# Start of a decoder layer on one Trainium2 core: the keys' weight ahead of half the tokens, exchanges ahead of the second keys, key groups in another order

## The chip, the cores and the metric

The kernel runs on one core of one Trainium2 chip. The metric is the device time of one execution in microseconds. The numbers in the views below come from one profiled execution; its own time and the times of unprofiled runs stand in the table further down.

## The reference

The reference is one layer of a pre-norm decoder in float32, on x of 4 batches x 1024 tokens x 512 features: self-attention with 16 heads of 32 features and sigmoid gates, cross-attention to a context of 4 x 1024 x 384, and a small network, each added to its input. Only the start concerns the change. Cut to that:

```python
n = layernorm(x)                          # per token, over 512 features
inner = n @ Wi                            # "queries" of self-attention, 512 x 512
outer = n @ Wo                            # "keys", 512 x 512
v = n @ Wv                                # values, 512 x 512
aperture, expression = sigmoid(n @ Wa + ba), sigmoid(n @ We + be)
a = softmax(inner @ outer.T / sqrt(32)) * aperture * expression
x = x + rotate((a / a.sum(-1)) @ v) @ Wout
x = x + cross_attention(layernorm(x), ctx) ; x = x + network(layernorm(x))
```

## The kernel before, in words

All engines work from instruction lists whose order is written out by hand in the program: the order in which Python issues operations is the order on each engine. Waits between engines are placed by the framework from the tiles that instructions read and write. SyncE (SP) and ScalarE (ACT) each issue transfers on a queue of their own, GpSimd (POOL) on a third.

Work is cut into batches of 1024 tokens, halves of 512 tokens and tiles of 128 tokens. Batch by batch, self-attention runs for every half and every group of four heads over eight key tiles; preparation of the next batch is woven between its steps. Ahead of the first attention step stands a list `first`, which has nothing to be woven into: it prepares batch 0 on its own. The change lies in that list and in the transfers ahead of it.

**Transfers.** `x0` holds tokens 0 to 511 as four tiles `xin`. Lines 135 to 137 ask for the four tiles, even ones on SP, odd ones on ACT. Lines 138 and 139 then ask for the keys' weight `wk0` (`attn_Wo`, 512 x 512) by quarters: `by_quarters` sends each quarter to 32 partitions, two quarters on SP and two on ACT. A tile and a quarter both are 256 KB.

**First half of batch 0.** For each tile, VectorE (DVE) takes statistics (L401, L402), GpSimd makes the scale 1/sqrt(variance + eps) (L405, L406), and VectorE normalizes in place (L303). VectorE's order is: statistics of 0 and 1, normalization of 0, statistics of 2, normalization of 1, statistics of 3, normalizations of 2 and 3. Then the tile is exchanged (`tr`, `across`, L325): TensorE (PE) multiplies 16 blocks with the identity into a PSUM bank `f`, of which there are two, and ScalarE copies the bank back over the tile (L331), so that features lie on partitions. ScalarE's first copy has the load of an activation table ahead of it.

**Keys of the first half.** `k_tiles(t0, nt, gs)` makes the keys of tiles t0 to t0 + nt - 1 for the groups gs of 128 output features, with 16 matmuls for each group (`columns`, L87), into `me["pk"][g]`. These four places are the halves of two PSUM tiles `s`: groups 0 and 1 share one, groups 2 and 3 the other. When the last tiles of a group are done, VectorE copies the group out to `k` (L284). `first_k` sets the order: tile 0's keys are cut into groups (0, 1) and (2, 3), and stand between exchanges; tiles 1 to 3 follow in one call with all four groups.

**After the keys.** SP's next transfer, tokens 512 to 1023 (L381), waits for a small GpSimd copy (L380) behind the scale of tile 3; behind it come the queries' weight `Wi` (`attn_Wi`) and the values' weight (`attn_Wv`). Then the query groups (`q`, L87 into `f`), gates (L482), and the values follow. The gates' weights (`attn_Wa`, `attn_We`) are asked for on ACT's queue behind the four exchange copies.

Of the kernel before, what the change touches and what calls it, by code (L numbers as in the profile page):

```python
# [10 lines left out]
F32 = mybir.dt.float32  # L11
# [5 lines left out]
P = 128  # L17
B, T, D = 4, 1024, 512
H, DH = 16, 32
NPR = H // 2  # L20
HG = 4
NT = T // P
NC = D // P
# [19 lines left out]
@with_exitstack  # L43
def decoder_kernel(ctx: ExitStack, tc: tile.TileContext, a: dict, out: bass.AP):

    nc = tc.nc
    keep = ctx.enter_context(tc.tile_pool(name="keep", bufs=1))
    flag = keep.tile([1, 1], I32, name="flag")
    E = mybir.EngineType
    with tc.manual_schedule(engines={E.PE, E.DVE, E.Activation, E.Pool, E.SP}):
        moderate_path(tc, a, out, flag)
    again = nc.values_load(flag[0:1, 0:1], min_val=0, max_val=1, skip_runtime_bounds_check_because="0 or 1")
    with tc.If(again > 0):  # L60
        general_path(tc, a, out)


def moderate_path(tc: tile.TileContext, a: dict, out: bass.AP, flag: bass.AP):
    nc = tc.nc
    x = a["x"]
    with ExitStack() as st:
# [6 lines left out]
        wp = enter(tc.tile_pool(name="mwp", bufs=3))  # L74
# [8 lines left out]
        def columns(to, lhsT, rhs, **flags):  # L83

            for j in range(4):
                r = slice(j * DH, (j + 1) * DH)
                nc.tensor.matmul(to[r], lhsT=lhsT[:, j, :] if len(lhsT.shape) == 3 else lhsT[:, r], rhs=rhs, **flags)  # L87

        def by_quarters(dma, to, w):

            for q in range(NC):
                dma[q * len(dma) // NC](to[ts(q, NB)], w.rearrange("(q c i) f -> q i c f", c=NC, i=NB)[q])
# [15 lines left out]
        for one, is_ in ((ones, 1.0), (power, -0.5), (share, 1.0 / M)):  # L108
# [6 lines left out]
        W_IN = {  # L115
            "q0": (a["attn_Wi"], NC), "k0": (a["attn_Wo"], NC), "v0": (a["attn_Wv"], NC),
            "q1": (a["xattn_Wq"], NC), "k1": (a["xattn_Wk"], NCK), "v1": (a["xattn_Wv"], NCK),
            "o1": (a["xattn_Wo"], NC),
        }
# [13 lines left out]
        x0 = p2.tile([P, 4, D], F32, tag="inT", name="xin")  # L133

        queues = [nc.sync.dma_start, nc.scalar.dma_start]
        for t in range(4):
            queues[t % 2](x0[:, t, :], x[0, t * P : (t + 1) * P, :])
        wk0 = wp.tile([P, NC, D], F32, tag="w", name="w")
        by_quarters(queues, wk0, W_IN["k0"][0])
        wae = const.tile([P, NC, 2 * H], F32, name="wae")  # L140

        nbae = const.tile([P, 1], F32, name="nbae")
# [133 lines left out]
        def evacuate(to, src, bias=None):  # L276

            if crossing:
                if bias is None:
                    nc.scalar.copy(to, src)  # L280
                else:
                    nc.scalar.activation(to, src, AF.Identity, bias=bias)
            elif bias is None:
                nc.vector.tensor_copy(to, src)  # L284
            else:
                nc.vector.tensor_scalar(to, src, bias, None, ALU.add)
# [48 lines left out]
        def chunk(xt, c, t0=0, n=4):  # L335

            return xt[:, t0 : t0 + n, :].rearrange("p t (s c j) -> p (t s) c j", c=NC, j=NB)[:, :, c, :]
# [18 lines left out]
        def pre(u):  # L356
# [72 lines left out]
            def tr(hf, t):  # L429
                def f():  # L430
                    if xt0(hf):
                        xn = me["xn", hf]
                        across(xn, t, first=True)
                    else:
                        xn = me["xT", hf]
                        blocks(xn, t)
                    me["in", hf] = lambda c: chunk(xn, c)
                    me["in", hf, "t"] = lambda c, i: chunk(xn, c, i, 1)
                return f
# [112 lines left out]
            def k_tiles(t0, nt, gs):  # L552

                def f():
                    xn = me["xn", 0]
                    if "pk" not in me:
                        me["pk"] = [two[:, i, :] for two in (ps.tile([P, 2, HALF], F32, tag="s", name="s") for _ in range(2)) for i in range(2)]
                        me["k"] = p2.tile([P, NC, T], F32, tag="k", name="k")
                    for g in gs:
                        to = me["pk"][g][:, t0 * P : (t0 + nt) * P]  # L560
                        for c in range(NC):
                            columns(to, me["wk"][:, c, ts(g, P)], chunk(xn, c, t0, nt), start=(c == 0), stop=(c == NC - 1))
                        if t0 + nt == 4:
                            evacuate(me["k"][:, g, 0:HALF], me["pk"][g])
                return [(1, f)]

            def first_k():
                trs_ = [[(1, tr(0, t))] for t in range(4)]
                return [
                    trs_[0], k_tiles(0, 1, (0, 1)), trs_[1], k_tiles(0, 1, (2, 3)), trs_[2], trs_[3],  # L570
                    k_tiles(1, 3, range(HG)),
                ]

            vs = [values(kt) for kt in range(NT)]
# [1188 lines left out]
```

## Time and profile before

| what | us |
|---|---|
| median of 3 runs | 2198.9 |
| the three runs | 2198.63, 2198.9, 2202.58 |
| profiled execution, its own time | 2197.95 |
| span of the profiled execution | 2196.1 |
| TensorE busy in the span | 2169.3 |
| first query group starts, from the span's start | 29.26 |
| first attention step starts | 102.14 |

All times in the views count from the start of the span. A line of a timeline gives start, length, engine, source line, operation, written and read tiles, shape and count; a bracket tells how long the engine was idle before it and which instruction or transfer released it. "x32" counts matmuls as the chip records them: a float32 matmul appears twice. The length of a run of matmuls reaches to the modelled end of the last one, so that the next run starts 0.2 us or so before that; starts are the safer numbers. "SPq" and "ACTq" lines are the issuing of transfers, not their landing. Line numbers are those of the kernel before; in the changed kernel all lines behind the edited transfers (from 140 on) are one higher.

### The profile page before, as it was taken

How to read it: one execution, taken by the hardware profiler on the slowest of the kernel's cores; microseconds unless marked ns; L12 is line 12 of the kernel's file. 1: busy time of each engine (PE TensorE's matmuls, PEld its weight loads, DVE VectorE, ACT ScalarE, POOL GpSimd, SP SyncE). 2: the span in 40 equal slices, each digit the busy share in tenths (PEclk: the TensorE clock that was granted, in tenths of full speed). 3: DMA queues.
4: the chain of work that ended last, by engine and by line, in shares of the span. 5: the costliest groups of instructions: out<-in, count | busy, mean ns of one | idle time of the engine just before them, and what ended most of it. 6: DMA issues, size and time to landing. Idle time of an engine off the chain costs nothing.

```text
span 2196.1 us, 53076 instructions
## 1 busy us (share of the span) xinstructions
PE 2169.3 (99%) x22750; PEld 556.2 (25%) x22750; DVE 1558.7 (71%) x2510; ACT 1240.3 (56%) x1493; POOL 85.6 (4%) x127
## 2 busy tenths in 40 slices
PE   8999999999999999999999999999999999999996
PEld 4322222222222222222222222222222222222223
DVE  3578675796757957567676676877777777856477
ACT  0155545555455554555656666675757666577673
POOL 2000000030200000000000000000000000000000
PEclk9999999999999999999999999999999999999998
DMA  5412133031340221211222132221233142202131
GB/s 153 134 47 72 47 98 113 19 89 66 97 118 19 85 66 51 74 47 42 69 85 90 45 93 65 79 76 53 69 86 110 50 103 69 81 19 80 60 89 41
DMA packets 154137, 161.72 MB, mean 74 GB/s; under 512 B 47002, under 2 KB 92698, under 8 KB 152740
## 3 DMA queue, kind: packets, MB, share of 16 engines
q1 hardware_dynamic: 149828, 156.14, 24.5%
q8 instruction: 180, 2.95, 0.6%
q0 software_dynamic: 2080, 0.98, 0.3%
q10 hardware_dynamic: 1984, 1.12, 0.2%
q14 instruction: 65, 0.53, 0.1%
HBM read 115.40 MB, written 42.74 MB: 72 GB/s over the span
## 4 chain that ended last, share of the span: by engine, by line
PE 95%; DVE 2%; ACT 1%; issue 1%; DMA 0%; ACTq 0%; DVEq 0%
PE f L87 36%; PE s L607 26%; PE av L634 22%; PE sm L642 6%; PE sm L664 3%; ACT e L612 1%; PE s L87 1%; PE f L912 1%; PE f L874 1%; DVE g L901 1%; DVE es L620 0%; DMA w<-in_attn_Wo 0%; PE f L482 0%; PE s L912 0%; PE f L325 0%
## 5 line engine op out<-in xcount | busy, mean ns | idle before, releaser
L612 ACT ACTIVATE e<-s 128x1024 f32<-128x1024 f32 x1024 | 993.6, 1022 | 709.6 <-PE s L607 511.7
L620 DVE TENSOR_TENSOR es<-es,e 128x1024 f32<-128x1024 f32 x534 | 642.4, 1227 | 268.3 <-ACT e L612 266.4
L607 PE MATMUL s<-q,k 32*64 32x512 f32 x8192 | 607.2, 613 | 2.2 <-ACT e L612 0.5
L634 PE MATMUL av<-e,v 128*32 128x512 f32 x4096 | 550.2, 603 | 0.0
L87 PE MATMUL f<-xT,w 128*32 128x512 f32 x2816 | 333.7, 592 | 0.0
L628 DVE SCALAR_TENSOR_TENSOR eg<-e,sw,eg 128x512 f32<-128x512 f32 x448 | 318.5, 747 | 2.3
L618 DVE TENSOR_TENSOR es<-e 128x1024 f32<-128x1024 f32 x89 | 106.8, 1223 | 219.9 <-ACT e L612 188.0
L607 PEld LDWEIGHTS s<-q,k 32*64 32x64 f32 x8192 | 132.8, 129 | 445.8 <-ACT e L612 241.4
L87 PE MATMUL f<-w,q 128*32 128x512 f32 x1984 | 240.3, 592 | 0.0
L634 PEld LDWEIGHTS av<-e,v 128*32 128x32 f32 x4096 | 87.9, 108 | 403.9 <-issue 401.3
L87 PEld LDWEIGHTS f<-xT,w 128*32 128x32 f32 x2816 | 92.1, 110 | 210.5 <-issue 206.0
L642 PE MATMUL sm<-e,sw 128*2 128x512 f32 x1024 | 133.3, 592 | 0.0
L87 PE MATMUL f<-w,xT 128*32 128x512 f32 x896 | 106.0, 592 | 0.6 <-DVE q L284 0.6
L87 PEld LDWEIGHTS f<-w,q 128*32 128x32 f32 x1984 | 65.5, 110 | 149.1 <-issue 142.6
L87 PE MATMUL f<-w,ctxT 128*32 128x512 f32 x768 | 92.6, 592 | 0.0
L87 PE MATMUL f<-ctxT,w 128*32 128x512 f32 x768 | 92.3, 592 | 0.0
L895 ACT ACTIVATE hid<-sT,units 128x256 f32<-128x256 f32 x128 | 76.5, 605 | 27.8 <-DVE g L901 24.1
L811 POOL TENSOR_TENSOR r<-res,bo_bc 128x512 f32<-128x512 f32 x32 | 40.9, 1279 | 1040.8 <-DVE res L803 703.4
L901 DVE SCALAR_TENSOR_TENSOR g<-hid,units,g 128x256 f32<-128x256 f32 x120 | 57.5, 480 | 14.2 <-ACT hid L895 9.1
L664 PE MATMUL sm<-es,fixed 128*1 128x512 f32 x348 | 65.0, 591 | 0.0
L803 DVE TENSOR_TENSOR res<-f,res 128x512 f32<-128x512 f32 x62 | 42.5, 686 | 15.5 <-PE f L87 11.6
L714 DVE TENSOR_TENSOR q<-both,recb 128x512 f32<-128x512 f32 x63 | 43.2, 686 | 6.7 <-DMA recb<-rec_d 6.7
(265 smaller groups left out, 1047.0 us busy)
## 6 DMA issues: line engine op xcount, KB each, us to landing
recb<-rec_d SPq DMA_DIRECT2D x252, 64.0 KB
xT<-rows_d SPq DMA_DIRECT2D x60, 256.0 KB
rows_d<-r SPq DMA_DIRECT2D x60, 256.0 KB
w<-in_xattn_Wo SPq DMA_DIRECT2D x9, 1024.0 KB
w<-wout_d SPq DMA_DIRECT2D x8, 1024.0 KB
res<-in_x SPq DMA_DIRECT2D x32, 256.0 KB
x1b_d<-r SPq DMA_DIRECT2D x32, 256.0 KB
res<-x1b_d SPq DMA_DIRECT2D x32, 256.0 KB
```

Source lines behind the costliest of these rows:

```text
L87: nc.tensor.matmul(to[r], lhsT=lhsT[:, j, :] if len(lhsT.shape) == 3 else lhsT[:, r], rhs=rhs, **flags)
L607: nc.tensor.matmul(s[m : m + 64, j, :], lhsT=k[r, g, kt * P + m : kt * P + m + 64], rhs=q[r, g, :], start=True, stop=True,)
L612: nc.scalar.activation(e, s, AF.Exp, scale=SCALE)
L618: nc.vector.tensor_tensor(me["es"][i], me["e", 0][i], es[i], ALU.add)
L620: nc.vector.tensor_tensor(me["es"][i], me["es"][i], es[i], ALU.add)
L628: nc.vector.scalar_tensor_tensor(eg, es[0][:, h, :], gate(kt), eg, ALU.mult, ALU.add)
L634: nc.tensor.matmul(av[r, :], lhsT=me["v"][:, kt, HG * g + h, :], rhs=es[h // 2][:, h % 2, :], start=(kt == 0), stop=(kt == NT - 1),)
L642: nc.tensor.matmul(sm[j * DH : j * DH + sums, :], lhsT=me["sw"][:, t, HG * g + 2 + h, :] if ph == 0 else ones, rhs=me["e", t][1][:, h, :], ...
L664: nc.tensor.matmul(sm[j * DH : j * DH + 1, :], lhsT=ones, rhs=e, start=True, stop=True)
L714: nc.vector.tensor_tensor(me["q", hf][:, g, :], both[:, 0, :], all_, ALU.mult)
L895: nc.scalar.activation(hid, res["s"], AF.Relu, bias=units[:, 1, h : h + 1], scale=units[:, 0, h : h + 1])
L901: nc.vector.scalar_tensor_tensor(res["g"], res["hid"], units[:, 2, h - 1 : h], res["g"], ALU.mult, ALU.add)
```

## The change

The weight's four quarters are asked for between token tiles 1 and 2, so that on each queue the order is token tile, two quarters, token tile. In `first_k` the exchanges of tiles 2 and 3 come before the second half of tile 0's keys. The last call makes the groups in the order 0, 2, 1, 3. VectorE's copies of the finished groups follow that order; nothing else in any engine's list is moved, added or removed.

```diff
         queues = [nc.sync.dma_start, nc.scalar.dma_start]
+        wk0 = wp.tile([P, NC, D], F32, tag="w", name="w")
         for t in range(4):
+            if t == 2:
+                by_quarters(queues, wk0, W_IN["k0"][0])
             queues[t % 2](x0[:, t, :], x[0, t * P : (t + 1) * P, :])
-        wk0 = wp.tile([P, NC, D], F32, tag="w", name="w")
-        by_quarters(queues, wk0, W_IN["k0"][0])
...
                 return [
-                    trs_[0], k_tiles(0, 1, (0, 1)), trs_[1], k_tiles(0, 1, (2, 3)), trs_[2], trs_[3],
-                    k_tiles(1, 3, range(HG)),
+                    trs_[0], k_tiles(0, 1, (0, 1)), trs_[1], trs_[2], trs_[3], k_tiles(0, 1, (2, 3)),
+                    k_tiles(1, 3, (0, 2, 1, 3)),
                 ]
```

## The prediction

> **What bounds the kernel now.** I read the page first: the engine table, then the chain that ended last.
>
> ```profile
> PE 2169.3 (99%) x22750; PEld 556.2 (25%) x22750; DVE 1558.7 (71%) x2510; ACT 1240.3 (56%) x1493; POOL 85.6 (4%) x127
> PE 95%; DVE 2%; ACT 1%; issue 1%; DMA 0%; ACTq 0%; DVEq 0%
> ```
>
> TensorE's instruction stream sets the end. The change adds no instruction to it and removes none, so it can only move the gaps in that stream. Then I read TensorE's timeline of the first 45 us (start, length, operation, and in brackets the idle time before it with its releaser), because the edits touch nothing later:
>
> ```profile
> 6.51 1.08 PE L325 MATMUL f<-ident,xin 128*32 128x128 f32 x32 [0.49 <-DVE xin L303]
> 9.86 1.96 PE L87 MATMUL s<-xin,w 128*32 128x128 f32 x64 [2.27 <-DMA w<-in_attn_Wo]
> 11.60 1.08 PE L325 MATMUL f<-ident,xin 128*32 128x128 f32 x32
> 12.47 1.96 PE L87 MATMUL s<-xin,w 128*32 128x128 f32 x64
> 14.22 1.96 PE L325 MATMUL f<-ident,xin 128*32 128x128 f32 x64
> 16.87 2.79 PE L87 MATMUL s<-xin,w 128*32 128x384 f32 x32 [0.69 <-ACT xin L331]
> 20.47 5.37 PE L87 MATMUL s<-xin,w 128*32 128x384 f32 x64 [0.81 <-DVE k L284]
> 26.65 2.79 PE L87 MATMUL s<-xin,w 128*32 128x384 f32 x32 [0.81 <-DVE k L284]
> 29.26 10.48 PE L87 MATMUL f<-xin,w 128*32 128x512 f32 x96
> ```
>
> Read from the starts: exchange of tile 0 (E0) at 6.51; first half of tile 0's keys (A) at 9.86 after 2.27 us of waiting for its weight; E1 11.60; second half (B) 12.47; E2 and E3 from 14.22; the four key groups of tiles 1 to 3 from 16.87, with two stops for a VectorE copy; first query group at 29.26. From 29.26 on TensorE is nearly gapless, so I take **the start of the query groups as the yardstick**. Next, VectorE in the same stretch:
>
> ```profile
> 6.37 0.69 DVE L401 BATCH_NORM_STATS2 bnst<-xin 128x6 f32<-128x512 f32 x1
> 7.19 0.52 DVE L303 TENSOR_SCALAR xin<-xin,bnmv,rs 128x512 f32<-128x512 f32 x1
> 8.47 0.55 DVE L303 TENSOR_SCALAR xin<-xin,bnmv,rs 128x512 f32<-128x512 f32 x1
> 9.78 0.66 DVE L303 TENSOR_SCALAR xin<-xin,bnmv,rs 128x512 f32<-128x512 f32 x1 [0.77 <-POOL rs L406]
> ```
>
> Here the reader sees tile 2's statistics at 6.37 and the normalizations of tiles 1, 2 and 3 after it. That tile 1's normalization stands behind tile 2's statistics in VectorE's order matters below. Last, windows with the transfers (last two columns: share of the 16 DMA engines, GB/s), and SyncE's queue:
>
> ```profile
> 3.50:5.00 1.50, 1.50 (x9) 1.50 (x9) 0.98 (x3) 0.00 (x0) 0.01 (x1) 1.00 1.04 387
> 7.00:8.40 1.40, 0.59 (x24) 0.32 (x12) 1.33 (x5) 1.39 (x2) 0.95 (x2) 1.00 0.97 293
> 8.40:9.00 0.60, 0.00 (x0) 0.00 (x0) 0.60 (x2) 0.02 (x1) 0.42 (x2) 1.00 0.15 38
> ```
>
> ```profile
> 10.02 0.39 SPq L381 DMA_DIRECT2D xin<-in_x  x1
> 10.46 2.65 SPq L92 DMA_DIRECT2D w<-in_attn_Wi  x4
> 18.88 7.68 SPq L92 DMA_DIRECT2D w<-in_attn_Wv  x4
> ```
>
> Tokens move at 387 GB/s, the weight's quarters at 293; the engines are full until 8.4 and then run out.
>
> [...] bytes end between 8.4 and 9.0, the weight's waiter goes on at 9.83. [...] here 1.28 us, from 6.54, in front of ScalarE's first copy.
>
> **The change part by part.**
>
> *Part 1, the weight ahead of tiles 2 and 3.* No DMA is added; on each queue one 256 KB token load is issued after two 256 KB quarters, about 0.9 us later by the issue times (1.66 to 2.56). Bytes: tiles 0 and 1 (0.52 MB) are in by about 3.5, as now. The weight's 1.05 MB at 293 GB/s take 3.6 us, to 7.1; with a receipt of 0.8 to 1.4 us it is usable at 7.9 to 8.5. A also needs E0's copy on ScalarE, which starts at 7.83 behind the table load, takes 0.59 us and ends at 8.42. So A starts at about 8.5, 1.4 us earlier. But tiles 2 and 3 now come last: 0.52 MB at 387 GB/s is 1.35 us, to 8.5 (8.7 with stragglers); with a lag between 0.5 us (tile 0: bytes 3.5, statistics 3.99) and 1.1 us, tile 2's statistics start at 8.9 to 9.8. I take **9.4, against 6.37 now: 3.0 us later**. Queued behind that wait on VectorE is tile 1's normalization, though tile 1 landed long before. From the statistics to E3's start I keep today's spacing: tile 3's normalization ends at 9.78 + 0.66 = 10.44 and TensorE follows a normalization by 0.05 (6.46 to 6.51), so 10.49 - 6.37 = 4.12. E1 comes at about 9.4 + 1.34 + 0.05 = 10.8, E2 at 12.1, **E3 at 13.5**. A's early start is thus lost in a new wait for E1.
>
> *Part 2, all exchanges ahead of B.* An exchange costs 0.87 (11.60 to 12.47), A or B 1.74. With part 2 alone, E1 stays at 11.60, E2 is at 12.47 and E3 at 13.38 (it needs E1's bank, copied from 12.74 to 13.33). B follows at 14.25, the groups at 16.0: E3's copy on ScalarE (0.59, after E3's 1.08) lies wholly beside B's 1.74, so the 0.69 wait goes, and 16.87 - 16.0 = **0.87 gained**. With part 1 too, E3 is at 13.5 instead of 13.38, so **part 1 costs 0.1** net (between a gain of 0.4 and a loss of 0.5 for statistics at 8.9 and 9.8).
>
> *Part 3, groups 0, 2, 1, 3.* Groups 0 and 1 are the halves of one PSUM tile, 2 and 3 of another; today group 1 stops for group 0's copy out, group 3 for group 2's. A group without a stop is 26.65 to 29.26 = 2.61. Four are 10.44; today they take 29.26 - 16.87 = 12.39. In the new order the group between is 2.61 long and covers the copy (0.06 to start, 0.69 long). **Gain 1.95**. Both copies hide under groups 2 and 1; VectorE has nothing else then.
>
> *Sum.* Query groups start at 13.5 + 0.87 + 1.74 + 10.44 = 26.55, against 29.26: **2.7 us earlier**.
>
> *What follows on the queues.* SyncE's load of tiles 4 to 7 waits for a GpSimd copy behind tile 3's scale (9.81, 3.4 after the statistics), so it and the query weight (`Wi`) slip 3.0, from 10.02 to about 13.0. Today those 2.1 MB fill the engines to about 19.5, with a receipt 20 to 21; then 23 to 24, against a need at 26.55: hidden, with 2.5 us or more left of today's 8 to 9. The value weight (four issues from 18.88, last ending 26.56) and the gates' weights on ScalarE's queue (from 16.94, last issue 27.1) slip likewise by up to 3; values are needed at 45.0 - 2.7, gates at 39.6 - 2.7, so at least 5 us remain. If that cover is gone, TensorE waits just as long as they are late. Later waits hang on TensorE or VectorE and shift with them.
>
> The profiled execution took 2197.95 with a span of 2196.1; a span of 2193.4 gives 2195.3. The median of the runs shown is 0.95 above that execution, so **2196.2**.
>
> **The rivals.**
>
> *Tokens hardly late (0.24).* [...] nothing but A holds E1: A 8.5, E1 10.2, E2 11.1, E3 12.0 (E1's bank) and queries at 25.05: 4.2 us, 2194.7. [...] Since this is the ceiling of the whole change, passing 4.4 us takes some spread of the measurement besides.
>
> *The query weight becomes the wait (0.08, slower).* SyncE's loads start late and share the engines with the gates' small transfers, issued at 15.4 instead of 16.94, so more of them beside the weight. The transfers from 15.0 to 19.0 already run at 190 to 270 GB/s with full engines. It decides from a landing at 26.55; from 29.26 the change loses, and at 34 by 4.7 us: 2203.6. Against it: 2.5 us of cover before the first microsecond counts.
>
> *The change doesn't do what it says (0.08).* If the copy out still stops the next group, because the wait goes by something other than the shared tile, part 3 brings nothing: 0.8 gained, 2198.1. Speaking against it: today group 2 follows group 1 with no stop (5.37 us in one piece from 20.47).
>
> **How the numbers follow.** The likeliest case has 0.60: statistics at 8.9 to 9.8 give 3.2 to 2.3 us, 2195.7 to 2196.6, and 0.3 for the runs' spread. The range for 8 in 10 takes in the ceiling (2194.7, less 0.3) and the no-gain case with some of the late weight: **2194.4 to 2199.2**. A measurement of this kernel can tell about 0.2% (4.4 us) from no change. The likeliest and the third case lie inside that; of the first rival I put 0.16 beyond it, by spread; of the second 0.08 if it is long. Faster 0.16, same 0.76, slower 0.08.
>
> **What would show it.** Right: A at about 8.5 with ScalarE or the weight as releaser; tile 2's statistics waiting for DMA until about 9.4; E1, E2 and E3 each released by VectorE; no ScalarE or VectorE wait in the groups; queries at 26 to 27. Wrong: queries released by `Wi`; statistics before 8 or after 11; a group waiting for a copy; or gaps after 30 us that are not there today.

## The result, and the profile after

| | before | changed |
|---|---|---|
| median, 22 runs each, us | 2198.7 | 2195.9 |
| lowest to highest, us | 2195.19 to 2202.58 | 2192.59 to 2197.61 |
| span of the profiled execution, us | 2196.1 | 2193.9 |
| query groups start, us | 29.26 | 26.50 |
| first attention step starts, us | 102.14 | 99.40 |

The ratio of the changed kernel's time to that of before is 0.9984, with a 95% interval of 0.9977 to 0.999: 2.8 us less by the medians, 0.13%. That is clear of the noise, but by the medians and by the ratio inside the 0.2% that the prediction took as the bound of no change; the interval reaches to 0.23%. The forecast was 2196.2.

TensorE's timeline of the changed kernel (start, length, operation, idle time before it with its releaser) is the view to put beside the one of before:

```profile
6.74 1.08 PE L326 MATMUL f<-ident,xin 128*32 128x128 f32 x32 [1.04 <-DVE xin L304]
8.70 1.95 PE L87 MATMUL s<-xin,w 128*32 128x128 f32 x64 [0.88 <-ACT xin L332]
10.83 1.08 PE L326 MATMUL f<-ident,xin 128*32 128x128 f32 x32 [0.18 <-DVE xin L304]
12.14 1.08 PE L326 MATMUL f<-ident,xin 128*32 128x128 f32 x32 [0.23 <-DVE xin L304]
13.56 1.08 PE L326 MATMUL f<-ident,xin 128*32 128x128 f32 x32 [0.34 <-DVE xin L304]
14.43 12.28 PE L87 MATMUL s<-xin,w 128*32 128x128 f32 x192
26.50 10.51 PE L87 MATMUL f<-xin,w 128*32 128x512 f32 x96
```

Three things are to be seen. The first keys start at 8.70, no longer released by the weight but by ScalarE's copy. Each of the next three exchanges has a short stop in front of it, released by VectorE. And from 14.43 the second half of tile 0's keys and all four groups run as one piece of 12.28 us, with neither the ScalarE wait nor the two VectorE waits. VectorE's timeline tells why the exchanges are spaced as they are:

```profile
9.35 0.69 DVE L402 BATCH_NORM_STATS2 bnst<-xin 128x6 f32<-128x512 f32 x1 [2.66 <-DMA xin<-in_x]
10.17 0.51 DVE L304 TENSOR_SCALAR xin<-xin,bnmv,rs 128x512 f32<-128x512 f32 x1
12.76 0.65 DVE L304 TENSOR_SCALAR xin<-xin,bnmv,rs 128x512 f32<-128x512 f32 x1 [0.77 <-POOL rs L407]
```

Tile 2's statistics wait 2.66 us for their tokens and start at 9.35 (6.37 before). Tile 1's normalization stands behind them, at 10.17, though GpSimd had its own scale ready at 7.11. The last line is tile 3's, held by GpSimd's scale.

The 2.76 us gained at the query groups are still 2.74 at the first attention step. The profiled spans differ by 2.2 only: this one execution had a stop of 0.27 us for ScalarE near 1678 us that the one of before had not, and its end ran differently: in the last 31 us of both the granted TensorE clock fell to 0.50 more than once, first for 6.8 us from 2165.6 in the one of before and for 3.4 from 2164.9 in the changed one. The medians are the better measure of the whole, the start of the trace that of the parts.

### The profile page after: what moved, and what is told of

The parts are those of the page before. It is cut to its first block, busy times and chain, and to the rows that moved or that the text cites. A ratio compares the mean times of both kernels' runs of the same rounds, so it can differ in the third digit from the quotient of the medians.

```text
span 2193.9 us, 53076 instructions
## 1 busy us (share of the span) xinstructions
PE 2168.4 (99%) x22750; PEld 557.5 (25%) x22750; DVE 1558.3 (71%) x2510; ACT 1240.3 (57%) x1493; POOL 85.3 (4%) x127
## 4 chain that ended last, share of the span: by engine, by line
PE 94%; DVE 2%; ACT 1%; issue 1%; DMA 1%; SPq 0%; POOL 0%; DVEq 0%; ACTq 0%
PE f L87 36%; PE s L608 25%; PE av L635 21%; PE sm L643 6%; PE sm L665 3%; ACT e L613 1%; DVE es L621 1%; PE f L913 1%; PE f L875 1%; PE s L87 1%; DVE g L902 1%; DMA xin<-in_x 0%; PE f L483 0%; PE s L913 0%; ACT hid L896 0%
```

## The experiments

The time of a single execution of this kernel varies by several us (57 executions of before that stand beside experiments e7 to e10 lie between 2194.16 and 2204.05), so an experiment with a single execution is read by its start alone (e1 to e6, e11 and e12), and only where there are 13 runs or more is a time compared (e7 to e10).

### Part 3 alone (e1_groups)

```diff
-                    k_tiles(1, 3, range(HG)),
+                    k_tiles(1, 3, (0, 2, 1, 3)),
```

> Part 3 alone: key groups in the order 0, 2, 1, 3, all else as before. Theory (a group only stops for the copy out of its PSUM tile's other half): both 0.81 us waits on the VectorE copy are gone, groups still start at 16.9, query groups at 29.26 - 1.95 = 27.3. Rival (the stop has another cause, such as the copy engine's turn): two stops of about 1 us remain and the query groups stay at 29.2.

TensorE's timeline of this kernel:

```profile
17.07 10.53 PE L87 MATMUL s<-xin,w 128*32 128x384 f32 x128 [0.69 <-ACT xin L331]
27.42 10.48 PE L87 MATMUL f<-xin,w 128*32 128x512 f32 x96
```

The four groups are one piece and take 10.35 us from start to start, against 12.39: part 3 is worth 2.04. Neither of the two stops of 0.81 us for VectorE's copy is left: they came from the copy out of the other half of the same PSUM tile, and the case that part 3 does nothing falls.

### Part 2 alone (e2_exchanges)

```diff
-                    trs_[0], k_tiles(0, 1, (0, 1)), trs_[1], k_tiles(0, 1, (2, 3)), trs_[2], trs_[3],
+                    trs_[0], k_tiles(0, 1, (0, 1)), trs_[1], trs_[2], trs_[3], k_tiles(0, 1, (2, 3)),
```

> Part 2 alone: exchanges of tiles 2 and 3 ahead of the second half of tile 0's keys, all else as before. Theory: exchange 3 at 13.4, second half at 14.25, groups at 16.0 with no wait on ScalarE, query groups at 28.4 (0.87 earlier). Rival (the exchanges pile up on the two banks or on ScalarE's copies): groups at 16.9 or later, query groups at 29.3.

Query groups started at 30.39, later than before. By itself that would fit the rival, but the loss lies ahead of the edit: the first keys, which this edit doesn't touch, took 3.29 us instead of 1.96 (the granted TensorE clock was 0.50 from 10 to 13 us). From exchange 1 (13.39) to the query groups it is 17.00, against 17.66 before: 0.66 gained where 0.87 was expected, and the wait on ScalarE is gone. Why 0.2 is missing was not followed up. This is inconclusive on the total; the next experiments settle part 2.

### Parts 2 and 3, part 1 undone (e3_both_orders, e9_both_orders_again)

The edits of e1 and e2 together, transfers as before. The first time:

> Parts 2 and 3, with the transfers as before: part 1 undone. Theory (part 1 is worth nothing net, since VectorE's turn behind the late tile 2 takes back what the early weight gives): exchange 3 at 13.4, query groups at 26.4, as in the changed kernel (26.50) within 0.3 us. Rival (the early weight is where a good part of the gain is from): exchange 3 at 14.8 or later, query groups at 27.5 to 27.9.

Here the clock fell again. TensorE's timeline, and then windows around the fall (columns: stretch, its length, busy time of PE, PEld, DVE, ACT and POOL with counts, granted clock, share of the DMA engines, GB/s):

```profile
10.11 3.42 PE L87 MATMUL s<-xin,w 128*32 128x128 f32 x64 [2.43 <-DMA w<-in_attn_Wo]
13.34 2.85 PE L325 MATMUL f<-ident,xin 128*32 128x128 f32 x96
```

```profile
6.35:9.76 3.41, 1.33 (x35) 0.94 (x33) 2.61 (x7) 1.87 (x2) 2.59 (x5) 1.00 0.60 163
9.76:13.17 3.41, 3.06 (x60) 3.09 (x64) 0.64 (x1) 0.00 (x0) 0.34 (x2) 0.50 0.48 176
```

From 9.76, still inside the stop for the weight, to 13.17 the granted clock is 0.50, and the first keys take 1.5 us more. Query groups started at 28.07, near what the rival expected, for a reason that neither theory named. So the same kernel was taken once more, with times:

> Parts 2 and 3 with the transfers as before, once more. In the first look at it the granted TensorE clock was 0.50 for 3.4 us from 9.8 on, right behind the 2.4 us in which TensorE waited for the weight, and the first keys took 3.42 us instead of 1.96. Theory (the clock falls in some executions behind that idle stretch[...]; part 1 is worth what it saves of this, and nothing else): either first keys at 1.96 and query groups at 26.2 to 26.5, or first keys near 3.3 and query groups near 28. Rival (the order itself makes the keys slow): query groups near 28 in any case, with a granted clock of 1.00 as well. Time: 2.0 to 2.8 us below before.

```profile
9.45 1.95 PE L87 MATMUL s<-xin,w 128*32 128x128 f32 x64 [1.32 <-DMA w<-in_attn_Wo]
11.19 2.86 PE L325 MATMUL f<-ident,xin 128*32 128x128 f32 x96
13.87 12.25 PE L87 MATMUL s<-xin,w 128*32 128x128 f32 x192
25.93 10.48 PE L87 MATMUL f<-xin,w 128*32 128x512 f32 x96
```

This time the clock stayed at 1.00 and the weight came earlier. TensorE has no gap behind the first keys: 16.48 us from their start to the query groups, against 19.40 before and 17.36 in e1. Part 2 is thus worth 17.36 - 16.48 = 0.88, as predicted. With the weight at 9.86, as in the profile of before, query groups would start at 26.34, an estimate: the changed kernel's 26.50 is no better. Over 21 runs the ratio to before is 0.9985 (0.9979 to 0.9992), median 2195.14: 3.2 us below the median of the 57 executions of before beside it, where 2.0 to 2.8 were expected. **Part 1 undone, the whole gain remains.**

### Part 1 alone (e4_weight_first)

```diff
+            if t == 2:
+                by_quarters(queues, wk0, W_IN["k0"][0])
```

> Part 1 alone: the weight ahead of tiles 2 and 3, the orders of exchanges and groups as before. Theory: first keys at 8.7, exchange 1 waits for VectorE until 10.8, second half at 11.7, exchanges 2 and 3 from 13.4 with no VectorE wait (the second half covers it), groups at 16.1, query groups at 28.5: 0.8 earlier alone, though nothing in company with part 2. Rival (late tiles cost more than the early weight gives): query groups at 29.3 or later. Rival (the full 1.2 to 1.4 us of the earlier first keys goes through): 27.9 to 28.1.

```profile
8.68 1.96 PE L87 MATMUL s<-xin,w 128*32 128x128 f32 x64 [0.88 <-ACT xin L332]
10.78 1.08 PE L326 MATMUL f<-ident,xin 128*32 128x128 f32 x32
11.65 1.96 PE L87 MATMUL s<-xin,w 128*32 128x128 f32 x64
13.39 1.96 PE L326 MATMUL f<-ident,xin 128*32 128x128 f32 x64
28.43 10.48 PE L87 MATMUL f<-xin,w 128*32 128x512 f32 x96
```

Query groups at 28.43, 0.83 earlier than before: of the 1.18 us by which the first keys start earlier, 0.35 go into the stop ahead of exchange 1. Alone, part 1 gains, because the second half of the keys covers the late tiles 2 and 3. Part 2 takes that cover away and replaces it with its own gain. The 0.83 is from one profile, in which tile 2 came early (statistics at 9.29); in e11 they came at 10.19 and exchange 1 at 11.68, later than the 11.60 of before, so the gain of part 1 alone hangs on that arrival.

### Which wait takes the early weight back (e5_norm1_early, e6_split)

```diff
-                    return [stats(0), stats(1), norm(0), stats(2), norm(1), stats(3), norm(2), norm(3)]
+                    return [stats(0), stats(1), norm(0), norm(1), stats(2), stats(3), norm(2), norm(3)]
```

> The changed kernel with one edit on VectorE: tile 1 is normalized ahead of tile 2's statistics. Theory (the wait of exchange 1 is only tile 1's place behind tile 2's arrival; exchange 3 is held by GpSimd's scale of tile 3, which hangs on the arrival too): exchange 1 follows the first keys without a VectorE wait, at first keys + 1.74; exchange 3 comes 3.4 to 3.7 after the statistics of tile 2 instead of 4.2; query groups at most 0.5 us earlier than in the changed kernel. Rival (exchange 1's wait is passed on in full): query groups not earlier at all.

Exchange 1 followed the first keys at once (10.76 behind 9.02). Tile 2's statistics started at 9.48 and the query groups at 26.13, 16.65 later; in the changed kernel it is 26.50 - 9.35 = 17.15. So VectorE's order costs 0.5. Tile 3's normalization, which still waited 0.46 us for GpSimd's scale, came 2.91 behind tile 2's statistics, where it was 3.41 in the changed kernel: the same 0.5.

```diff
-                    trs_[0], k_tiles(0, 1, (0, 1)), trs_[1], trs_[2], trs_[3], k_tiles(0, 1, (2, 3)),
+                    trs_[0], k_tiles(0, 1, (0, 1)), trs_[1], k_tiles(0, 1, (2,)), trs_[2], trs_[3], k_tiles(0, 1, (3,)),
```

> The changed kernel with one edit on TensorE: group 2 of tile 0's keys behind exchange 1, group 3 behind exchange 3. Theory (the holes ahead of exchanges 2 and 3 are about 0.45 us each and can hold group 2's 0.87): exchange 3 still 4.2 after tile 2's statistics, groups of tiles 1 to 3 start 0.8 us earlier behind exchange 3 (1.8 instead of 2.6), query groups 0.7 to 0.8 us earlier than in the changed kernel for the same arrival of tile 2. Rival (group 2 pushes exchanges 2 and 3 back by its own length): query groups as in the changed kernel.

```profile
10.91 1.08 PE L326 MATMUL f<-ident,xin 128*32 128x128 f32 x32 [0.18 <-DVE xin L304]
11.78 1.08 PE L87 MATMUL s<-xin,w 128*32 128x128 f32 x32
12.65 2.07 PE L326 MATMUL f<-ident,xin 128*32 128x128 f32 x64
25.77 10.48 PE L87 MATMUL f<-xin,w 128*32 128x512 f32 x96
```

Statistics at 9.42, query groups at 25.77: 16.35 later, 0.80 less than the changed kernel's 17.15. Group 2 fits into the holes between the exchanges.

### Both together (e7_split_norm1), and the changed kernel again (e10_after_again)

> The changed kernel, with two more edits: tile 1 is normalized ahead of tile 2's statistics, and the second half of tile 0's keys is cut in two, group 2 behind exchange 1 and group 3 behind exchange 3. Theory (VectorE's turn behind tile 2 holds exchange 1; GpSimd's scale of tile 3 holds exchange 3; holes between exchanges can be filled): exchange 1 at 10.4, group 2 at 11.3, exchange 2 at 12.2, exchange 3 at 13.2, groups of tiles 1 to 3 at 14.9 right behind ScalarE's copy, query groups at 25.4, 1.1 earlier than the changed kernel, if the queries' weight has landed. Rival (the queries' weight, 2 us of cover or less in the changed kernel): query groups released by that transfer at 26 or later. Time: 3 to 4 us below before.

```profile
9.27 1.96 PE L87 MATMUL s<-xin,w 128*32 128x128 f32 x64 [1.45 <-DMA w<-in_attn_Wo]
11.01 1.08 PE L326 MATMUL f<-ident,xin 128*32 128x128 f32 x32
25.76 10.48 PE L87 MATMUL f<-xin,w 128*32 128x512 f32 x96
```

In this profile the weight came at 9.27 and was again what the first keys waited for; from there TensorE had no gap (16.49 to the query groups). The query groups came at 25.76, short of the expected 25.4 because of this weight, not of the queries' weight. The ratio to before is 0.998 (0.9972 to 0.9988, 15 runs, median 2194.48): 3.9 us less, as expected (3 to 4).

> The changed kernel once more, beside the others on one chip: query groups at 26.5, granted clock 1.00 from 6 to 16 us, time 2.7 us below before within 1; if the clock theory holds, its start is the same in every look, while kernels that wait for the weight vary by 1.4.

The changed kernel beside it: median 2195.96 over 19 runs, 2.4 us below before, ratio 0.9989 (0.9983 to 0.9996). Its statistics of tile 2 came at 9.91, exchange 3 at 14.13 and the query groups at 27.07: the spacing of 4.22 held, the arrival moved by 0.56. The expectation that its start is the same every time was wrong. The version with both edits has the lowest median of all; its interval and that of the changed kernel overlap slightly.

### Idle matmuls in the wait for the weight (e8_keep_warm)

```diff
+            def keep_warm():
+                idle = bank()
+                for i in range(8):
+                    nc.tensor.matmul(idle[:, 0:P], lhsT=ident, rhs=ident, start=True, stop=True)
...
+                    trs_[0], [(0, keep_warm)], k_tiles(0, 1, (0, 1)), trs_[1], trs_[2], trs_[3], k_tiles(0, 1, (2, 3)),
```

> Parts 2 and 3 with the transfers as before, and eight idle 128x128 matmuls on the identity in the wait for the weight, behind exchange 0. Theory (idle TensorE is what lets the clock fall): the granted clock is 1.00 from 6 to 16 us, first keys 1.96 long from about 10.0, query groups at 26.4; no idle stretch over 1 us. Rival[...]: a stretch at 0.50 can show all the same, with first keys near 3.3. Rival (the idle matmuls are in the way): first keys at 10.5 or later.

The clock was 1.00 and the first keys took 1.95, from 10.30, with 0.31 us of waiting for the weight left. But one execution at full clock tells little, as four of the six profiles with the weight last and no idle matmuls show the first keys at full speed too (1.95 or 1.96), and over 13 runs the kernel can't be told from before (ratio 0.9996, 0.9988 to 1.0004; median 2196.96). Why it is slower than the same kernel without them is open. This profile doesn't show it at the start, where the query groups began at 26.79, 2.5 us ahead of before.

### The cover of the queries' weight taken away (e11_values_first)

```diff
-        first = ... + p["x"][1] + ahead(0, "q")
-        first += one(load_gates) + ahead(0, "v") + ...
+        first = ... + p["x"][1] + ahead(0, "v")
+        first += one(load_gates) + ahead(0, "q") + ...
```

> The changed kernel with the values' weight asked for ahead of the queries' weight on SyncE's queue, so that the cover of the latter is gone on purpose. Theory (late weight turns into a TensorE wait one for one): groups end at 26.5 as in the changed kernel, the queries' weight lands near 30, query groups start then with a DMA wait of 3 to 4 us, and everything after is late by that. Rival (there is more cover than the issue times show): query groups at 26.5 to 27 without a DMA wait.

TensorE's timeline, and windows of the stop and of what comes behind it:

```profile
32.56 13.06 PE L87 MATMUL f<-xin,w 128*32 128x512 f32 x96 [5.00 <-DMA w<-in_attn_Wi]
```

```profile
27.50:32.50 5.00, 0.06 (x4) 0.00 (x0) 2.99 (x7) 0.00 (x0) 0.00 (x0) 0.84 0.60 157
32.50:42.00 9.50, 9.44 (x65) 2.77 (x69) 2.84 (x12) 0.00 (x0) 0.00 (x0) 0.72 0.01 2
```

TensorE waits 5.0 us, more than the 3 to 4 expected, and three query groups then take 13.06 us instead of 10.5. The clock went to 0.50 during the stop and stood there for about 6.9 us in all, by the means of the two windows (0.84 over 5.0 us, 0.72 over 9.5). The first attention step started at 108.02, and in the changed kernel at 99.40. As tile 2 came later in e11, the cost is counted from the second half of tile 0's keys: 92.74 us (15.28 to 108.02) against 84.97 (14.43 to 99.40, and the same in e10). **A stop of 5.0 us cost 7.8**: 2.6 of it lie behind the stop, in the query groups (12.87 us from their start to the gates, against 10.30).

### The kernel before again (e12_before_again)

> The kernel before, a second look at its start: first keys between 9.4 and 10.3, behind the weight; query groups 19.4 later (29 to 29.7) if the granted TensorE clock stays at 1.00 behind the wait, 1.4 more if it falls to 0.50 for 3.4 us. No theory is at stake; it tells how much the start of one kernel varies from look to look.

First keys at 9.90 and 1.95 us long (1.96 in the first profile of before, at a clock of 1.00); query groups at 29.30. Besides e8, six profiles are of kernels in which the weight comes last (the two of before, e1, e2, e3, e9): the first keys started between 9.45 and 10.29, and in two of the six the clock fell. In the seven profiles with part 1 (the changed kernel twice, e4 to e7, e11) the first keys took 1.95 or 1.96, and the granted clock was 1.00 from 1.4 to 17 us in the changed kernel both times, in e4 and in e7.

## Why the prediction was right, and where it was not

**Arrival of tile 2: right, the closeness by luck.** Statistics were forecast for 9.4 and came at 9.35; the wait in front of tile 1's normalization was there, and exchange 3 came 4.21 after them (forecast 4.12), at 13.56 (13.5). That tiles 2 and 3 would land behind the weight, as they are asked for, was the author's estimate; the changed kernel bears it out for tile 2: the first keys had the weight at 8.70, and tile 2 released VectorE at 9.35. In the other profiles with part 1 the statistics came at 9.29 to 10.19, twice outside the 8.9 to 9.8 that the prediction allowed (9.91 in e10, 10.19 in e11); the spacing to exchange 3 held (4.22 in both), and what moved was the arrival.

**First keys: right in the releaser.** ScalarE's copy, at 8.70 instead of 8.5, because tile 0 itself came 0.23 later. The prediction had the first tiles "as now", but tile 0's statistics started at 4.21 or 4.22 in three profiles with part 1 (the changed kernel twice, e7) and at 3.99 to 4.17 in three without it (before, e8, e9). In four of the seven (e5, e7, e10, e11) the weight was the releaser, at 9.02 to 9.52, so the first keys did not come at 8.5 there.

**Parts 2 and 3: right.** 0.88 for 0.87 and 2.04 for 1.95. The sum of 2.7 was measured as 2.76 at the query groups; in the second profile of the changed kernel (e10) it was 2.2, as tile 2 came 0.56 later.

**Part 1 costs 0.1: right within what can be told.** e9 shows that nothing is lost by undoing it; e3, in which the clock fell, can't tell. That it gains 0.83 alone was not said, nor that its late tiles make the holes that e6 fills.

**The query weight's cover: the step that failed.** It read "23 to 24, against a need at 26.55: hidden, with 2.5 us or more left". The queue of the changed kernel:

```profile
13.44 9.25 SPq L92 DMA_DIRECT2D w<-in_attn_Wi  x4
```

The last of the four quarters was issued at 22.39, after SyncE had waited 7.1 us; before, it was issued at 12.7 without such a wait. The profile names a gates' transfer (`wae<-in_attn_Wa`) of ScalarE's queue as what ended the wait. In e5 and e6 the four issues took 8.50 and 7.68 us, in e4, with the transfers asked for in the same order, only 2.78. So what this issue waits for stays open. The working moved the issues as a block and did not ask what a single one waits for. By the transfers' records the bytes of this quarter ended at 24.72. Before, TensorE went on 0.8 us after the last bytes of the keys' weight (9.07 and 9.86). In e11 the last bytes of the queries' weight lie between 31 and 32 us, and TensorE went on at 32.56, 0.6 to 1.6 later. The prediction calls this lag a receipt; what it consists of is not shown, only its length. By the lag of 0.8 us the changed kernel's weight was usable near 25.5, an estimate, which leaves about 1 us of cover where 2.5 or more was forecast. Nothing waited for it, but the rival was nearer than the working had it.

**"TensorE waits just as long as they are late": wrong in size.** The clock added to it, 7.8 for 5.0 in e11. The prediction took every TensorE gap at its length; gaps of 2.63 and 2.43 us cost 1.4 and 1.5 us more in e2 and e3, while one of 2.46 in e1 did not.

**What stays open:** how often the clock falls at the start of the kernel before, and what decides it (last section). Two of six at 1.4 to 1.5 us each would be half a us on average in favour of part 1, but the 21 runs of e9 are not slower than the 19 of the changed kernel beside them (2195.14 and 2195.96).

## What to carry to other kernels

Before moving a transfer ahead, follow what moves behind it. Here VectorE waited for tile 2 until 9.35 and held tile 1's normalization behind that wait to 10.17, though its scale was ready at 7.11; the first keys' early start (8.70) ended in later stops (0.18, 0.23 and 0.34 us ahead of the three exchanges). Two accumulations that share one PSUM tile are better written with another one between them, so that the copy out of the first is covered (2.04 us here, for two such pairs). And price a stop of TensorE above its length: here two of the three stops of 2.4 to 2.6 us cost 1.4 and 1.5 us more, and the one of 5.0 cost 2.8 more. Price a queue of transfers by each issue's own wait (7.1 us for one quarter here).

## What the runs showed of the hardware that was not expected

The granted TensorE clock fell to 0.50 in stops of 2.43 and 2.63 us, and stayed at 1.00 through one of 2.46. The longest stops ahead of the first attention step, by length:

| profile | stop, waiting for | length, us | granted clock then |
|---|---|---|---|
| before | keys' weight | 2.27 | 1.00 |
| e12 | keys' weight | 2.31 | first keys took 1.95, as at 1.00 |
| e3 | keys' weight | 2.43 | 0.50 for 3.4 us, from 9.76 |
| e1 | keys' weight | 2.46 | 1.00 |
| e2 | keys' weight | 2.63 | 0.50 for 3.4 us, from about 9.7 |
| e11 | queries' weight | 5.00 | 0.50 for about 6.9 us, from about 30.9 |

Each of the three falls began before TensorE went on (at 10.11, 10.29 and 32.56), so that the work behind the stop paid for it. In the other profiles, and in e11, TensorE stood for 0.31 to 1.54 us ahead of the first keys, and these took 1.95 or 1.96. The length of the stop alone does not decide: e1's was longer than e3's, and only e3 lost the clock. What decides between 2.3 and 2.6 us is not shown here.

When the transfers that are asked for in the first 3 us landed varied between executions: with the weight last, the first keys started from 9.45 to 10.29; with the tokens last, tile 2's statistics from 9.29 to 10.19.
